# A third buffer for the gathered rows of y, R shared out anew over the periods, and x1's zero padding on VectorE

## The chip, the cores and the metric

The kernel runs on one core of a Trainium2 chip. A core has five engines with a queue of instructions each: TensorE (PE in the profile; its weight loads, PEld, overlap the products), VectorE (DVE), ScalarE (ACT), GpSimd (POOL) and SyncE (SP, which here only issues transfers). They meet through semaphores. Transfers run on 16 DMA engines. The metric is the time of one execution in microseconds; the time before is the median of three runs, 1281.5 (1278.85 to 1284.95).

## The reference, cut to what matters

```python
# x: 2708 x 256, adj: 2708 x 2708, some 0.3% of it nonzero, float32
x  = layernorm(x + relu(concat([x, adj @ x]) @ weight + bias))        # layer 0
R  = adj + eye(2708);  R = R / R.sum(-1, keepdims=True)               # layer 1
Z, Xf, Xa = 0, x, x
for n in range(2):
    A  = top_p_attention(Xa, W1, W2, W3)   # softmax of (Xa W1' W2') (Xa W3')'; of each row
                                           # the largest 0.9 of the mass, scaled to sum 1
    Xf = R @ Xf
    Xa = A @ Xa
    Z  = Z + Xf @ U1[n].T + Xa @ U2[n].T
x  = layernorm(x + layernorm(x + Z))
```

So there are two dense attention steps, A of 2708 x 2708 each time, and a chain of two products with the sparse R. Since R(R x) U1[1]' + (R x) U1[0]' = R (R (x U1[1]') + x U1[0]'), the kernel first forms yf = x U1[1]' and v0 = x U1[0]', then v = R yf + v0, then R v, which goes into the sum.

## The kernel before, in words

**Blocks.** The 2708 rows are 22 blocks (NB) of 128; the last one (EDGE) has 20 rows. The 2708 columns of A or adj are turned and multiplied in chunks of 128.

**Layer 0** (to about 265 us) multiplies adj by x on TensorE, block by block (L266), and leaves x1, the layer's result, in SBUF. Meanwhile DVE and POOL make for each block a list of the columns of adj that hold a nonzero: at most 896, seven chunks of 128. `Lists.end` closes such a round: DVE orders the marks (up to L350), POOL writes them to memory, scatters them by seven indirect transfers (L354) and reads the list `ix` back (L357). There are two rounds, one before step 1 and one within it; for each block only the listed rows of adj' are then kept (adjc in memory, 7 chunks of 128 columns, and the block's own 128 x 128 piece).

**Just after the first round** stand two instructions for the last block of x1: POOL zeroes a 128 x 256 tile, `x1_edge` (L508), and DVE copies the 20 rows of x1 into it (L509). The products of step 1 read it as the 22nd chunk (`part_y`, L583), the first time at the last slot of turn 0. Then follow POOL's memset of `sums` (L603), read by `finish1`.

**Step 1** is a software pipeline over blocks t. Logits of a block (PE L527) go through one PSUM buffer and are copied to one of four row buffers `e` by ACT (L534). DVE takes each segment's largest 8 (`extract1`, L589) and sorts them; ACT takes exponentials (`exps1`: first of the sorted values, L630, then of the row); DVE finds the threshold and zeroes what lies below (`finish1`, L654). `begin1` starts three blocks, with `u1_project` between, which makes yf and v0 with TensorE and U1, copies them out on ACT (L673) and stores them; it is the last reader of U1. Then the loop over t runs: in six slots each four transposes of `e` (PE L554, copied by ACT L556) and four products with x1 (PE L583), with exps1(t+2), finish1(t+1), logits and extract1 of t+3 beside them. The step's result goes on to q, k and za in memory; `ya_pair` (PE L691) makes ya = Xa U2[1]' at the end, and the first three blocks' logits of step 2 stand there too.

**Step 2** is a loop over periods `per` from 0 to 23 of six slots. In a period PE turns and multiplies block per-2 (again L554 and L583, now with ya), DVE searches the top-p threshold of blocks per and per-1 (L1045 is the one pass that ends the search's first part, L1110 the mask that releases the block to PE), ACT makes passes for block per+1 and exponentials of block per+2 (logits again L527). Everything is issued in the order of the code; each engine runs its own part in that order.

**R** is done within step 2, in units. One unit is one product of a chunk (PE L769), eight to a block: seven chunks of gathered rows and the block's own 128 rows. There are 176 units for yf (s = 0) and 176 for v (s = 1). `units` says how many go into each period: 16 first, 8 each in periods 0 and 1, 18 in each of 2 to 9, none in 10, 16 in each of 11 to 21. With a block's first unit `r_load` asks for the next block: adj's chunks by two SP transfers into one of three `adj` tiles (`a_load`), seven indirect gathers on POOL (`y_load`, L739), one chunk of 128 rows of 256 floats each, into the one of two buffers `yg` that the block before used, and the own rows by an SP transfer into the eighth place of the same buffer. The first two blocks' gathers are issued earlier, in the last-but-one turn of step 1 (`y_at`). With s = 0 the result is scaled and added by DVE (L797) and stored to v; after the last block v is complete and the gathers of s = 1 can start. With s = 1 the result is added to za (`arrive`).

**The finals.** A block whose three parts have arrived goes through two layernorms, `Final`, two blocks at a time (`final_slot`): statistics on DVE (L1204), roots on ACT (L1241), the first norm on ACT (L1214) into one of four spare tiles, then gain and x1 added on POOL (L1229, L1230), and a slot later statistics again. The last blocks, in `tail`, use DVE in POOL's place.

**Room.** One SBUF tile of 128 x 5416 floats, `y_room`, holds the two buffers of y (8 chunks each), the four spare tiles, and `x1_edge`.

Of the kernel before, what the change touches and what calls it, by code (L numbers as in the profile page):

```python
# [20 lines left out]
P = 128  # L21
# [18 lines left out]
ML = 16  # L40
CW, CC = 128, 7
AT = 96
# [19 lines left out]
def gnn_two_layer_kernel(ctx: ExitStack, tc: tile.TileContext, N, xT_d, x_d, adj_d, w0_d, b0_d,  # L62
# [45 lines left out]
    c.adj_d, c.out_d = adj_d, out_d  # L108
# [50 lines left out]
def fast_path(ctx, tc, c, flags, fint, xT_d, x_d, w0_d, b0_d, w1_d, w2_d, w3_d, u1_d, u2_d, g_d, b_d):  # L159
# [344 lines left out]
    YW = 2 * (CC + 1) * D  # L504
    yg = y_room[:, :YW].rearrange("p (s c d) -> p s c d", s=2, d=D)
    spares = [y_room[:, YW + D * i:YW + D * (i + 1)] for i in range(4)]
    x1_edge = y_room[:, YW + 4 * D:YW + 5 * D]
    nc.gpsimd.memset(x1_edge, 0.0)  # L508
    nc.vector.tensor_copy(x1_edge[AT:AT + rows(EDGE)], x1[:rows(EDGE), EDGE, :])  # L509
    lists = Lists(ML, NB, flags[:, NF - 2:], yg[:, 1].rearrange("p c d -> p (c d)"))  # L510
# [224 lines left out]
    def y_load(s, m):  # L735
        y = yg[:, m % 2]
        rows_d = (c.yf_d, c.v_d)[s].rearrange("p k d -> (p k) d")
        for i in range(CC):
            nc.gpsimd.indirect_dma_start(out=y[:CW, i, :], out_offset=None, in_=rows_d,  # L739
                                         in_offset=bass.IndirectOffsetOnAxis(ap=ix[:CW, m, i:i + 1], axis=0))  # L740
        y_in[s, m] = y
# [7 lines left out]
    def r_load(s, m):  # L749
        if m not in a_in:  # L750
            a_load(m)
        if (s, m) not in y_in:
            y_load(s, m)
        y = y_in.pop((s, m))
        nc.sync.dma_start(out=y[:rows(m), CC, :], in_=(c.yf_d, c.v_d)[s][:rows(m), m, :])
        r_in[s, m] = a_in.pop(m), y

    def r_units(n):
        for _ in range(n):
            s, m = r_queue[0]  # L760
            p = rows(m)
            if not r_now:
                r_now[:] = [ps_misc(), 0]
                if m + 1 < NB:
                    r_load(s, m + 1)
            acc, k = r_now
            a, y = r_in[s, m]
            kw = CW if k < CC else p
            nc.tensor.matmul(acc[:p, :D], lhsT=a[:kw, k, :p], rhs=y[:kw, k, :], start=k == 0, stop=k == CC)  # L769
# [24 lines left out]
    def r_out(s, m, acc, base):  # L794
        p = rows(m)
        if s == 0:
# [3 lines left out]
            if m == NB - 1:  # L800
                r_load(1, 0)
        else:
# [111 lines left out]
    y_at = {(NB - 2, 2): 0, (NB - 2, 5): 1}  # L914
    stores = []
    blocks = {}
    for t in range(NB):
# [5 lines left out]
        ra_next = finish1(t + 1) if t + 1 < NB else None  # L923
        for g in range(NG):
# [31 lines left out]
            if (t, g) == (NB - 1, 2):  # L956
                a_load(0)
# [6 lines left out]
    r_load(0, 0)  # L964
    for f in ends:
# [313 lines left out]
    first = 2 * (CC + 1)  # L1279
    units = {0: CC + 1, 1: CC + 1}  # L1280
# [117 lines left out]
def general_path(ctx, tc, c):  # L1398
# [15 lines left out]
    ps = ctx.enter_context(tc.tile_pool(name="gps", bufs=2, space=PSUM))  # L1414

# [341 lines left out]
```

## Time and profile before

| | |
|---|---|
| median of 3 runs | 1281.5 us (1278.85 to 1284.95) |
| the profiled execution: its time, its span | 1286.8, 1284.9 us |
| TensorE clock granted, mean | 0.975 |
| busy: PE, PEld | 1202.1 (94%), 904.3 us (70%) |
| busy: DVE, ACT, POOL | 973.9 (76%), 735.1 (57%), 634.9 us (49%) |
| gathers L739, yf and v | 154 each: 190.7 and 193.5 us busy, 48.3 and 59.3 idle before them |
| products of R, L769 | 704 records: 187.9 us busy, 18.1 idle before them |
| DMA | 165.99 MB, mean 129 GB/s |
| first transpose of step 1; R's first gather from step 2; end | 347.6; 744.4; 1284.9 us |

Times are microseconds from the start of the span. In a timeline a row is one instruction, or a run of like ones (x16): its start, its length, engine, line, operation, what it writes and reads, and in brackets the idle time of its engine before it with the instruction or transfer that ended it. A row of busy times by stretch gives the stretch, its length, the busy time and number of instructions of PE, PEld, DVE, ACT and POOL, then the granted clock, the DMA engines' share and GB/s. "issue" is idle time that no wait in the records explains.

### The profile page before, as it was taken

What the parts mean: (1) busy time and instruction counts of PE and PEld (TensorE: products, weight loads), DVE (VectorE), ACT (ScalarE), POOL (GpSimd) and SP (SyncE); (2) the same over time, 40 slices, a digit from 0 to 9 for tenths busy, and PEclk for the clock granted to TensorE, in tenths of its full rate; (3) what the DMA queues carried; (4) which work ended last, traced back from release to release, by engine and by line L of the source; (5) the groups of instructions that cost most, each with busy time, mean ns of one, the idle gap of its engine ahead of it and who ended that gap; (6) DMA issues with size and microseconds to landing.
All of it is one profiled execution on the core that took longest, in us unless ns stands there. A gap on an engine that the chain in (4) does not pass through costs nothing.

```text
span 1284.9 us, 18709 instructions
## 1 busy us (share of the span) xinstructions
PE 1202.1 (94%) x5772; PEld 904.3 (70%) x5772; DVE 973.9 (76%) x3253; ACT 735.1 (57%) x1299; POOL 634.9 (49%) x597
## 2 busy tenths in 40 slices
PE   8999999987799999999999978999998999999885
PEld 6888888842377777777777646777766777776664
DVE  2455554973999998988871278979878999999886
ACT  2000111032566666666665498887888999989821
POOL 1000000004076552577766068878774878888860
PEclk9999999989899999999999888999999999999997
DMA  7455544523322220133334154665664555555451
GB/s 197 149 197 172 160 151 153 172 82 98 100 80 92 61 68 32 41 94 94 91 89 107 50 152 152 181 187 178 183 150 122 173 160 163 169 185 160 144 135 39
DMA packets 101703, 165.99 MB, mean 129 GB/s; under 512 B 17362, under 2 KB 74070, under 8 KB 101594
## 3 DMA queue, kind: packets, MB, share of 16 engines
q1 hardware_dynamic: 75308, 108.65, 26.1%
q0 software_dynamic: 20544, 51.17, 14.8%
q10 hardware_dynamic: 5742, 4.89, 1.3%
q8 instruction: 48, 0.79, 0.3%
q14 instruction: 61, 0.50, 0.1%
HBM read 130.74 MB, written 33.90 MB: 128 GB/s over the span
## 4 chain that ended last, share of the span: by engine, by line
PE 71%; DVE 10%; ACT 7%; DMA 6%; issue 3%; POOL 2%; SPq 0%; POOLq 0%; ACTq 0%; DVEq 0%
PE acc L583 23%; PE acc L266 16%; PE lg L527 8%; PE misc L769 6%; PE tr L554 6%; DMA yg<-yf_d,ix 3%; PE acc L670 2%; DMA yg<-v_d,ix 2%; DVE e L1110 2%; PE misc L402 2%; ACT e L988 2%; PE acc L691 2%; PE misc L441 2%; PE misc L719 2%; PE acc L477 1%
## 5 line engine op out<-in xcount | busy, mean ns | idle before, releaser
L556 ACT COPY wT<-tr 128x512 f32<-128x512 f32 (+2 forms) x258 | 136.6, 537 | 205.8 <-PE tr L554 205.8
L583 PE MATMUL acc<-ya,wT 128*128 128x256 f32 x924 | 223.1, 383 | 0.0
L739 POOL DMA_INDIRECT yg<-v_d,ix x154 | 193.5, 1256 | 59.3 <-issue 25.3
L583 PE MATMUL acc<-x,wT 128*128 128x256 f32 x882 | 217.4, 386 | 0.0
L739 POOL DMA_INDIRECT yg<-yf_d,ix x154 | 190.7, 1239 | 48.3 <-issue 26.2
L266 PE MATMUL acc<-y,adj_t 128*128 128x257 f32 x924 | 206.1, 382 | 0.0
L769 PE MATMUL misc<-yg,adj_t 128*128 128x256 f32 (+1 forms) x704 | 187.9, 398 | 18.1 <-DMA yg<-yf_d,ix 7.2
L583 PEld LDWEIGHTS acc<-x,wT 128*128 128x128 f32 x882 | 159.0, 190 | 58.1 <-issue 24.7
L583 PEld LDWEIGHTS acc<-ya,wT 128*128 128x128 f32 x924 | 172.1, 191 | 38.2 <-issue 16.7
L266 PEld LDWEIGHTS acc<-y,adj_t 128*128 128x128 f32 x924 | 174.9, 191 | 27.3 <-issue 1.9
L376 POOL DMA_INDIRECT adj_t<-in_adj,ix x154 | 168.4, 1094 | 50.9 <-issue 39.5
L769 PEld LDWEIGHTS misc<-yg,adj_t 128*128 128x128 f32 (+1 forms) x704 | 123.6, 191 | 69.6 <-issue 23.2
L527 PE MATMUL lg<-k,q 64*128 64x512 f32 (+3 forms) x528 | 138.0, 600 | 27.4 <-ACT e L534 13.5
L554 PE MATMUL tr<-ident,e 128*128 128x128 f32 (+1 forms) x946 | 145.2, 272 | 6.9 <-ACT wT L556 4.6
L554 PEld LDWEIGHTS tr<-ident,e 128*128 128x128 f32 (+1 forms) x946 | 117.7, 141 | 40.5 <-ACT wT L556 8.8
L343 POOL DMA_DIRECT2D part_d<-e x1 | 0.6, 573 | 278.6 <-DVE e L342 278.6
L988 ACT ACTIVATE e<-e,st 128x2708 f32<-128x2708 f32 (+1 forms) x43 | 113.5, 2640 | 0.1
L991 ACT ACTIVATE e<-e,st 128x2708 f32<-128x2708 f32 (+1 forms) x42 | 111.0, 2642 | 0.1
L454 ACT COPY x1T<-tr 128x256 f32<-128x256 f32 (+1 forms) x22 | 8.0, 365 | 179.8 <-PE tr L453 179.8
L589 DVE MAX8 cand<-e 128x8 f32<-128x170 f32 (+1 forms) x352 | 86.9, 318 | 15.9 <-ACT e L534 15.7
L1052 DVE MAX8 cand<-w 128x8 f32<-128x170 f32 (+1 forms) x352 | 94.1, 321 | 0.0
L527 PEld LDWEIGHTS lg<-k,q 64*128 64x128 f32 (+1 forms) x528 | 39.3, 183 | 59.1 <-issue 20.7
(246 smaller groups left out, 1749.6 us busy)
## 6 DMA issues: line engine op xcount, KB each, us to landing
adj_t<-in_adj SPq DMA_DIRECT2D x44, 704.0 KB
adj_t<-adjc_d SPq DMA_DIRECT2D x44, 448.0 KB
adjc_d<-adj_t SPq DMA_DIRECT2D x22, 256.0 KB
base<-za_d SPq DMA_DIRECT2D x40, 128.0 KB
adjc_d<-adj_t SPq DMA_DIRECT2D x22, 192.0 KB
xt<-in_x ACTq DMA_DIRECT2D x21, 128.0 KB
x_d<-x SPq DMA_DIRECT2D x21, 128.0 KB
x1b_d<-xb SPq DMA_DIRECT2D x21, 128.0 KB
```

The costliest lines, as they stand in the source:

```text
L266: nc.tensor.matmul(acc[:p, :n], lhsT=halves[k // KH][:, k % KH, :p], rhs=y[:, k, :n], start=k == 0, stop=stop and k == NB - 1)
L376: nc.gpsimd.indirect_dma_start(out=a[:CW, i, :], out_offset=None, in_=adj_rows, in_offset=bass.IndirectOffsetOnAxis(ap=ix[:CW, m, i:i + 1] ...
L527: nc.tensor.matmul(lg[:p, h, at:at + b - a], lhsT=q[o, t * P:t * P + p], rhs=keys[s][o, i, :b - a], start=True, stop=True)
L554: nc.tensor.transpose(tr[:, k % 4, :p], columns(e[:p], k), ident[:p, :p])
L556: nc.scalar.copy(wT[:, :len(ks), :p], tr[:, :len(ks), :p])
L583: nc.tensor.matmul(acc[:p, :D], lhsT=wT[:, k % 4, :p], rhs=part_y(y, k), start=k == 0, stop=k == NB - 1)
L589: nc.vector.max(dst[:p, i * 8:(i + 1) * 8], src[:p, i * step:i * step + w])
L739: nc.gpsimd.indirect_dma_start(out=y[:CW, i, :], out_offset=None, in_=rows_d, in_offset=bass.IndirectOffsetOnAxis(ap=ix[:CW, m, i:i + 1], ...
L769: nc.tensor.matmul(acc[:p, :D], lhsT=a[:kw, k, :p], rhs=y[:kw, k, :], start=k == 0, stop=k == CC)
L988: nc.scalar.activation(scr[:b.p, :N], e, AF.Relu, bias=b.nz, scale=b.l[k], accum_out=b.relu)
L991: nc.scalar.activation(scr[:b.p, :N], e, AF.Sign, bias=b.nz, scale=b.l[k], accum_out=b.sign)
L1052: nc.vector.max(b.cand[:p, 8 * i:8 * i + 8], low[:p, SEG2 * i:SEG2 * (i + 1)])
```

## The change

- `yg` has three buffers of seven chunks instead of two of eight. With a block's first unit `r_load` asks for the block after the next. The own rows go to free chunks of the block's adj tile (chunks 8 and 9 of its 11), so `r_in` holds three things.
- The four spare tiles of the finals and `x1_edge` lie in U1's place, which step 1 leaves after `u1_project`. The kernel's other path (`general_path`, which is taken only when a list or a search overflows) loads U1 again.
- x1_edge's zeros are a DVE memset and stand, with the copy, in turn 0 of step 1 behind finish1(1).
- The gathers of the first three blocks of yf are issued in step 1, at other slots, and the first two adj loads there too; at the hand-over from s = 0 to s = 1 two blocks are asked for instead of one.
- Units: 24 first, 8 in period 0, 16 in period 1, 16 in each of periods 2 to 9, none in 10, 16 in each of 11 to 21.

```diff
--- before.py
+++ after.py
@@ -105,7 +105,7 @@
 
     c = Common()
     c.N, c.D, c.DA, c.NB, c.DC, c.KH, c.CHS, c.rows = N, D, DA, NB, DC, KH, CHS, rows
-    c.adj_d, c.out_d = adj_d, out_d
+    c.adj_d, c.out_d, c.u1_d = adj_d, out_d, u1_d
     c.x1_d = dram.tile([N, D], FP, name="x1_d")
     c.x1b_d = dram.tile([N, D], FP, name="x1b_d")
     c.za_d = dram.tile([N, D], FP, name="za_d")
@@ -501,13 +501,12 @@
     assert not weights
     lists.end()
     y_room = big.tile([P, DC * N], FP, tag="Y", name="yg")
-    YW = 2 * (CC + 1) * D
-    yg = y_room[:, :YW].rearrange("p (s c d) -> p s c d", s=2, d=D)
-    spares = [y_room[:, YW + D * i:YW + D * (i + 1)] for i in range(4)]
-    x1_edge = y_room[:, YW + 4 * D:YW + 5 * D]
-    nc.gpsimd.memset(x1_edge, 0.0)
-    nc.vector.tensor_copy(x1_edge[AT:AT + rows(EDGE)], x1[:rows(EDGE), EDGE, :])
-    lists = Lists(ML, NB, flags[:, NF - 2:], yg[:, 1].rearrange("p c d -> p (c d)"))
+    YW = CC * D
+    yg = y_room[:, :3 * YW].rearrange("p (s c d) -> p s c d", s=3, d=D)
+    idle = [c.u1[:, j, i, :] for j in range(DC) for i in range(2)]
+    spares = list(idle)
+    x1_edge = idle[0]
+    lists = Lists(ML, NB, flags[:, NF - 2:], y_room[:, YW:])
     lists.turn()
     x1_transpose(NB - 1)
     x1_qk(len(CHS) - 1)
@@ -733,7 +732,7 @@
     ready = []
 
     def y_load(s, m):
-        y = yg[:, m % 2]
+        y = yg[:, m % 3]
         rows_d = (c.yf_d, c.v_d)[s].rearrange("p k d -> (p k) d")
         for i in range(CC):
             nc.gpsimd.indirect_dma_start(out=y[:CW, i, :], out_offset=None, in_=rows_d,
@@ -751,9 +750,10 @@
             a_load(m)
         if (s, m) not in y_in:
             y_load(s, m)
-        y = y_in.pop((s, m))
-        nc.sync.dma_start(out=y[:rows(m), CC, :], in_=(c.yf_d, c.v_d)[s][:rows(m), m, :])
-        r_in[s, m] = a_in.pop(m), y
+        a, y = a_in.pop(m), y_in.pop((s, m))
+        own = a[:, CC + 1:CC + 1 + D // P, :].rearrange("p c i -> p (c i)")
+        nc.sync.dma_start(out=own[:rows(m)], in_=(c.yf_d, c.v_d)[s][:rows(m), m, :])
+        r_in[s, m] = a, y, own
 
     def r_units(n):
         for _ in range(n):
@@ -761,12 +761,13 @@
             p = rows(m)
             if not r_now:
                 r_now[:] = [ps_misc(), 0]
-                if m + 1 < NB:
-                    r_load(s, m + 1)
+                if m + 2 < NB:
+                    r_load(s, m + 2)
             acc, k = r_now
-            a, y = r_in[s, m]
+            a, y, own = r_in[s, m]
             kw = CW if k < CC else p
-            nc.tensor.matmul(acc[:p, :D], lhsT=a[:kw, k, :p], rhs=y[:kw, k, :], start=k == 0, stop=k == CC)
+            nc.tensor.matmul(acc[:p, :D], lhsT=a[:kw, k, :p], rhs=y[:kw, k, :] if k < CC else own[:p],
+                             start=k == 0, stop=k == CC)
             r_now[1] += 1
             if k == CC:
                 r_now.clear()
@@ -799,6 +800,7 @@
             nc.sync.dma_start(out=c.v_d[:p, m, :], in_=base[:p])
             if m == NB - 1:
                 r_load(1, 0)
+                r_load(1, 1)
         else:
             arrive(m, base, acc, rinv[:p, m:m + 1])
 
@@ -911,7 +913,7 @@
 
     at = {(m // 2, 3 * (m % 2) + 1): m for m in range(4)}
     at.update({(m - 2, 3): m for m in range(4, NB)})
-    y_at = {(NB - 2, 2): 0, (NB - 2, 5): 1}
+    y_at = {(NB - 3, 5): 0, (NB - 2, 3): 1, (NB - 1, 1): 2}
     stores = []
     blocks = {}
     for t in range(NB):
@@ -921,6 +923,9 @@
         if t >= NB - 3:
             b = blocks[t - (NB - 3)] = Block(t - (NB - 3))
         ra_next = finish1(t + 1) if t + 1 < NB else None
+        if t == 0:
+            nc.vector.memset(x1_edge, 0.0)
+            nc.vector.tensor_copy(x1_edge[AT:AT + rows(EDGE)], x1[:rows(EDGE), EDGE, :])
         for g in range(NG):
             turn(t, g, x1, acc, es[t % 4])
             if ends and 1 <= g <= 3:
@@ -953,8 +958,8 @@
             if (t, g) in y_at:
                 name_y()
                 y_load(0, y_at[t, g])
-            if (t, g) == (NB - 1, 2):
-                a_load(0)
+            if t == NB - 1 and 1 < g < 4:
+                a_load(g - 2)
         if t == EDGE:
             products(0)
             acc = edge_sum(acc, D, meanwhile=ya_pair)
@@ -962,6 +967,7 @@
         ra = ra_next
     assert not stores and not staged and not to_turn
     r_load(0, 0)
+    r_load(0, 1)
     for f in ends:
         ya_pair()
         f()
@@ -1276,8 +1282,8 @@
 
 
     each = NB * (CC + 1)
-    first = 2 * (CC + 1)
-    units = {0: CC + 1, 1: CC + 1}
+    first = 3 * (CC + 1)
+    units = {0: CC + 1, 1: 2 * (CC + 1)}
     rest = each - first - sum(units.values())
     units.update({p: rest * (p - 1) // 8 - rest * (p - 2) // 8 for p in range(2, 10)})
     units.update({p: each * (p - 10) // 11 - each * (p - 11) // 11 for p in range(11, 22)})
@@ -1413,6 +1419,9 @@
     small = ctx.enter_context(tc.tile_pool(name="gsmall", bufs=4))
     ps = ctx.enter_context(tc.tile_pool(name="gps", bufs=2, space=PSUM))
 
+    for s in range(2):
+        nc.sync.dma_start(out=u1[:, :, s, :], in_=c.u1_d[s].rearrange("(c p) e -> p c e", p=P))
+
     def ps_lg():
         return ps.tile([P, CH], FP, tag="lg", name="lg")
```

## Prediction

> **What bounds the kernel now.** I read, in this order: the busy slices and the chain of the page, the list of waits, the timelines of DVE, ACT, PE and POOL at 262–366 us and from 680 us on, and the busy time of the engines by period of step 2. TensorE is busy 94% of the span and holds 71% of the chain, so what counts is where it waits, and where it has more to do than the stage's other limit. Two places stand out.
>
> The first is the start of step 1, here in the timelines of POOL, DVE, ACT and PE (start, length, work, idle time before it and what ended that):
>
> ```profile
> 309.63 1.24 POOL L357 DMA_DIRECT2D ix<-list_d  x1 [1.41 <-DMA list_d<-e,to]
> 310.86 0.32 POOL L508 MEMSET yg<- 128x256 f32 x1
> ...
> 311.22 0.56 DVE L509 COPY yg<-x 20x256 f32<-20x256 f32 x1 [19.58 <-POOL xs L603]
> 311.79 3.88 DVE L589 MAX8 cand<-e 128x8 f32<-128x170 f32 x16
> ...
> 321.22 0.35 ACT L630 ACTIVATE srt<-srt,nmax 128x65 f32<-128x65 f32 x1 [12.88 <-DVE srt L596]
> ...
> 325.33 2.08 PE L527 MATMUL lg<-k,q 64*128 64x512 f32 x4 [12.96 <-ACT e L534]
> ```
>
> The zeroing L508 stands on POOL behind the first list's seven scatters (L354) and the read L357, which go one by one and end at 310.87. DVE has nothing else before its copy L509 and waits 19.6 us; its sort for block 0 (L589) comes after; ACT waits 12.9 us for the sort; PE waits 13.0 us for ACT to empty the one logits buffer.
>
> The second place is R in step 2. In POOL's timeline every gather L739 takes 0.95 and has 0.30 us before it, from 744 to 1245 us:
>
> ```profile
> 744.44 0.95 POOL L739 DMA_INDIRECT yg<-yf_d,ix  x1 [1.68 <-PE misc L769]
> 745.70 0.94 POOL L739 DMA_INDIRECT yg<-yf_d,ix  x1 [0.30 <-PE misc L769]
> ...
> 797.91 3.22 POOL L739 DMA_INDIRECT yg<-yf_d,ix  x1 [0.30 <-DMA yg<-yf_d,ix]
> ...
> 960.59 0.95 POOL L739 DMA_INDIRECT yg<-yf_d,ix  x1 [0.30 <-issue]
> 975.50 0.94 POOL L739 DMA_INDIRECT yg<-v_d,ix  x1 [13.97 <-DMA v_d<-base]
> ...
> 1042.82 0.73 POOL L1229 TENSOR_TENSOR yg<-yg,gb 128x256 f32<-128x256 f32 x1 [2.15 <-ACT yg L1214]
> ...
> 1241.07 0.73 POOL L1229 TENSOR_TENSOR yg<-yg,gb 128x256 f32<-128x256 f32 x1
> ```
>
> POOL stands still only at the hand-over from yf to v (14.0 us) and once before L1229 (2.15). It never waits for a free buffer. A gather costs 1.25 us, and two in each period (like that at 797.91) meet DVE's passes L1110 and L1045 and cost some 2.35 more. The stretches, by first transpose of a period (length, then busy PE, PE loads, DVE, ACT, POOL):
>
> ```profile
> 801.90:825.00 23.10, 23.10 (x115) 18.16 (x114) 20.95 (x77) 19.89 (x32) 18.53 (x16) 1.00 0.56 170
> 825.00:970.60 145.60, 141.55 (x679) 105.02 (x678) 121.94 (x418) 119.48 (x192) 109.72 (x89) 1.00 0.59 170
> 970.60:991.30 20.70, 17.02 (x84) 11.99 (x82) 16.57 (x52) 19.82 (x32) 12.44 (x12) 1.00 0.51 153
> 1013.60:1035.90 22.30, 22.30 (x112) 17.46 (x111) 20.91 (x75) 20.29 (x34) 18.04 (x15) 1.00 0.56 173
> ```
>
> Row 1 is a period with 18 units of R and nothing missing: PE needs 23.1. Row 2 is six more such periods of 24.3 each: POOL's 15.75 gathers x 1.25 + 2 x 2.35 = 24.4. Row 4 has 16 units: PE needs 22.3. From about 1130 us on POOL sets the pace again, through L1229/L1230 for which DVE waits:
>
> ```profile
> 1217.71 0.43 DVE L1204 BATCH_NORM_STATS2 bst<-yg 128x6 f32<-128x256 f32 x1 [2.15 <-POOL yg L1230]
> 1242.63 0.43 DVE L1204 BATCH_NORM_STATS2 bst<-yg 128x6 f32<-128x256 f32 x1 [2.77 <-POOL yg L1230]
> ```
>
> **Part 1, x1's zeros.** POOL loses one memset (0.32). DVE's sort can start when L350 is done and block 0's logits are copied, at 291.7 instead of 311.8, and ends at 301.1. ACT reaches L630 after its own copies, whose last one (L673) ends at 308.34: it starts there and not at 321.22, 12.8 us sooner. From there the order is a chain (ACT's exponentials, DVE's finish1 and second sort, ACT, the last projections, the first transpose at 347.57), each link as long as before, and step 1 is PE without a gap (34.0 busy of 34.0 in five stretches). So **-12.8** reaches step 2. PE's own wait shrinks to some 0.2 us. The `sums` memset L603, behind the same scatters, is done at 311.2 against a need at 311.6, so it doesn't bite; if it did, fractions of a us.
>
> The zeroing and copy come back in turn 0: a DVE memset of that size takes 0.27 (L182), the copy 0.56. They stand behind finish1(1), which ends near 352.4, after PE's last read of U1 (347.6), so their new wait is empty; if it weren't, block 3's sort and, through it, turn 3 would be late. Need for x1_edge: 364.7. Cover: finish1(1) is ready 10 us ahead of its turn. Without it, +0.8. Taken: 0. Spares in U1's place, own rows in adj's tile and the reload in the general path (not entered) change no instruction's size or number here. The waits for a free buffer on SP (own rows, 101 us in all, its longest 16.4) pass to adj's loads: behind them stand za's and v's stores and x1b's loads, but each load is now asked for two blocks (some 20 us) ahead, and PE waited only once for adj (0.97). Taken: 0; from 0 to +2.
>
> **Part 2, R anew.** *Before R.* Seven more gathers go out at 703.7 in POOL's 39 us of idle time: 7 x 1.25 = 8.8, hidden. Units move from periods 2–9 (18 to 16) into the opening burst (16 to 24) and period 1 (8 to 16), where ACT's passes set the pace. DVE's products of the burst now number three and wait for PE until 754, about 3.6 us later than now; ACT doesn't need them.
>
> *Where it pinches.* POOL's stream from 744.4 is saturated either way, so gather j now stands where gather j-7 stood. The end of period 1 takes 48 units, gather 42: the present 35th, issued at 776.6, landing near 780 (landings: median 3.6 after issue). Period 2's first five chunks are the present 36th to 40th, the last issued at 785.4, landing near 788.6; PE wanted them at about 783. So the logits behind them come at 789 instead of 783.6, +5.5. Two units fewer by then bring period 3 to 806.5 against 801.9: **+4.6** (from 0, if landings are quick, to +7).
>
> *Periods 3–9.* POOL could do 14 x 1.25 + 2 x 2.35 = 22.2, PE needs 22.3: seven periods at 22.3 = 156.1 against 168.7: **-12.6**. Two limits so close together cost something; I add +1 (0 to 4). Period 10 starts **7.0** sooner. Its 20.7 and the 14-us hand-over stay, since the last product, DVE's L797 and the store of v follow as now.
>
> *The way back.* In the second product POOL's order becomes 49 gathers, then the first L1229, where it was 42: +7 x 1.25 = 8.75, less the 2.15 of idle time that goes, = **+6.6**. So the first L1229 pair stands at 1042.8 - 7.0 + 6.6 = 1042.4, as now, though DVE arrives sooner: it waits about 2 us for the pair in period 13 and is bound to POOL from there. The pairs keep their 24.8 us (14 gathers, 4 x 0.75, two slow ones). Up to 1219 us nearly all of the 7 is gone: **-0.4**.
>
> *Tail.* After the eighth pair only 7 gathers remain instead of 14; PE's waits for chunks at 1224–1234 and DVE's 2.77 + 0.84 at 1242 go. Period 21 takes about 21.5 (DVE busy 21.0) instead of 24.9: **-3.4**.
>
> **Two rules weighed.** Row: gathers of 3.2 where others take 0.95. The Trainium skill, "SBUF — State Buffer", section "Who interferes with whom": DVE with two SBUF inputs and a GpSimd instruction that reads SBUF share a port, and the second blocks until the first is done. L1110 and L1045 have two such inputs, a gather reads its list. Counted as full passes of 3.05, POOL would need 14 x 1.25 + 2 x 3.05 = 23.6 in periods 3–9, and those would yield -3.5 rather than -12.6; period 10 would even start late and the sum be -6. The six periods of row 2 bear out 2.35, which I take. The skill's first page ("Trainium Kernel Development and Optimization", "Best Practices") has buffering hide transfers behind compute; by it PE's 14.4 us of waits for gathers would all go on top of -12.8, a sum of -27. The rows speak against it: a producer that never waits for a buffer gains only a head start.
>
> **Sum:** -12.8 - 0.4 - 3.4 = -16.6. Profiled: span 1284.9, execution 1286.8, so 1.9 lie around it. 1286.8 - 16.6 = 1270.2; the execution shown is 5.3 above the median of 1281.5, so against that **1265**. No change and change are told apart here from about 0.5%, 6.4 us.
>
> **Rivals.**
> - *Gathers land early enough* (0.22): no stall in period 2. For it: POOL's lead of six gathers today at 780; against: that lead is what the move spends. Period 10 11.6 sooner instead of 7.0: -21, about 1260; with a lighter coupling of POOL and DVE 1256.
> - *Step 2 gives nothing* (0.25): landings of up to 6.3 us and POOL's 22.2 against PE's 22.3 make PE stall; period 10 only 2 sooner, so +4.6 at the eighth pair and -3.4 after it. -12.8 + 1.2: about 1270; 1274 with period 10 unmoved and a smaller tail.
> - *The zeros were not the cause* (0.06): DVE still waits near 291, for a list transfer that the view names badly. Against: L350 ends at 291.6. Only -3.8: 1278.
> - *Slower* (0.04): a ring in periods 13–20. L1230 late, so DVE's mask late, PE late, the buffer of three blocks ago late, POOL idle, the next L1230 later still. It decides once POOL stands still over 2.9 us in each of eight periods, 23 us in all: from there the time passes 1288, say 1290. Against: that buffer is released about a period before its gather.
>
> **Numbers.** 0.43 for 1265 and the rest as given. The middle case alone spans 1261 to 1269. Range 1255 to 1276: the two neighbours with their bounds, leaving out the last two cases and the far edges. Faster 0.89, same 0.07, slower 0.04.
>
> **What would show it.** Part 1: no DVE wait before the first sort, the first transpose near 334.8, step 2's R near 730.7. Part 2: in period 2 a PE wait for gathers of some 5 us; periods 3–9 at 22.3 to 22.6; the hand-over's POOL gap still near 14; L1204 waiting for L1230 from the first pair on, pairs 24.8 apart; no PE wait for gathers after 1150. I'd be wrong if periods 3–9 stay near 24, if pairs come closer than 24.8, or if the first transpose moves by less than 12.

## The result, and the profile after

| | before | after |
|---|---|---|
| median, us | 1282.3 (1278.9 to 1285.0) | 1268.4 (1264.8 to 1270.3) |
| ratio after / before | | 0.9891, 95% interval 0.9863 to 0.9920 |
| profiled execution: its time, its span | 1286.8, 1284.9 | 1264.8, 1263.0 |
| granted TensorE clock, mean | 0.975 | 0.987 |

The kernel became 13.9 us faster; 1265 was forecast. The two profiled executions differ by 21.9 us, more than the medians, because that of before lay 5 us above its median and that of after 4 us below its own; a second trace of the changed kernel, taken beside the experiments, has a span of 1265.7. Two of the four sets of experiments ran where the kernel before itself takes 1326 us and ACT, in the traces, stands still for up to 28.6 us with no wait in the records that explains it; kernels from there are compared only with each other.

The start of step 1, in the timelines of POOL, DVE, ACT and PE of the changed kernel (start, length, work, idle time before it and what ended that), and the same two rows of PE in the kernel before:

```profile
306.63 1.24 POOL L357 DMA_DIRECT2D ix<-list_d  x1 [1.40 <-DMA list_d<-e,to]
307.87 0.11 POOL L602 MEMSET xs<- 128x1 f32 x1
...
288.73 0.21 DVE L350 SCALAR_TENSOR_TENSOR to<-run,before_m,e 16x7 int32<-16x7 f32 x1
288.87 3.86 DVE L588 MAX8 cand<-e 128x8 f32<-128x170 f32 x16
...
307.60 0.35 ACT L629 ACTIVATE srt<-srt,nmax 128x65 f32<-128x65 f32 x1
...
328.49 5.46 PE L669 MATMUL acc<-u,x1T 128*128 128x512 f32 x8 [4.20 <-ACT v_out L672]
333.87 0.66 PE L553 MATMUL tr<-ident,e 128*128 128x128 f32 x4
```

```profile
342.11 5.46 PE L670 MATMUL acc<-u,x1T 128*128 128x512 f32 x8 [2.40 <-ACT v_out L673]
347.50 0.66 PE L554 MATMUL tr<-ident,e 128*128 128x128 f32 x4
```

DVE goes from the list (L350) straight into the sort; its 19.6 us of waiting there are gone (it waits 10.2 for ACT's exponentials later), and so are ACT's 12.9 ahead of the exponential (L629 now) and PE's 13.0. The list itself is nearly as late as it was (L357 ends at 307.87 instead of 310.87): DVE, ACT and PE no longer stand behind it. The first transpose stands at 333.9 instead of 347.5.

Step 2 by stretches (length, busy PE, PE loads, DVE, ACT, POOL, granted clock, DMA share, GB/s): period 3, periods 4 to 9, period 10, period 12, period 14 of the changed kernel:

```profile
790.85:813.24 22.39, 22.39 (x112) 17.35 (x111) 18.19 (x64) 19.88 (x32) 18.12 (x15) 1.00 0.60 182
813.24:946.68 133.44, 133.44 (x657) 102.13 (x656) 119.63 (x413) 119.33 (x192) 98.63 (x79) 1.00 0.56 160
946.68:967.33 20.65, 16.98 (x84) 11.96 (x82) 18.27 (x60) 19.78 (x32) 11.25 (x10) 1.00 0.54 173
989.64:1011.92 22.28, 22.28 (x112) 17.45 (x111) 20.89 (x75) 20.28 (x34) 18.02 (x15) 1.00 0.57 174
1036.92:1061.08 24.16, 22.77 (x111) 17.29 (x111) 22.08 (x80) 22.27 (x38) 19.87 (x19) 1.00 0.55 170
```

Periods 4 to 9 take 133.44 / 6 = 22.24 us and PE is busy for all of it; before they took 24.3. From period 14 on a period is 24.2 us with PE busy 22.8. POOL's timeline around the hand-over from yf to v, at the finals' first pair and at their eighth, and two of DVE's waits, show what paces that part:

```profile
934.69 0.95 POOL L738 DMA_INDIRECT yg<-yf_d,ix  x1 [0.30 <-issue]
953.34 0.94 POOL L738 DMA_INDIRECT yg<-v_d,ix  x1 [17.70 <-PE tr L553]
...
1027.99 0.75 POOL L1235 TENSOR_TENSOR u<-u,gb 128x256 f32<-128x256 f32 x1
...
1197.96 0.73 POOL L1235 TENSOR_TENSOR u<-u,gb 128x256 f32<-128x256 f32 x1
...
1029.57 0.43 DVE L1210 BATCH_NORM_STATS2 bst<-u 128x6 f32<-128x256 f32 x1 [3.40 <-POOL u L1236]
1031.07 0.43 DVE L1210 BATCH_NORM_STATS2 bst<-u 128x6 f32<-128x256 f32 x1 [0.86 <-POOL u L1236]
```

POOL stands still for 17.7 us at the hand-over (14.0 before), then for no more than 0.43 us at a time until its last gather at 1213.1, and DVE waits for the finals' additions (L1236) from the first pair on.

### The profile page after: what moved, and what is told of

It reads as the page before. It is cut to its first block, busy times and chain, and to the rows that moved or that the text cites. A ratio compares the mean times of both kernels' runs of the same rounds, so it can differ in the third digit from the quotient of the medians.

```text
span 1263.0 us, 18675 instructions
## 1 busy us (share of the span) xinstructions
PE 1191.0 (94%) x5772; PEld 901.6 (71%) x5772; DVE 969.5 (77%) x3254; ACT 734.8 (58%) x1299; POOL 631.5 (50%) x596
## 4 chain that ended last, share of the span: by engine, by line
PE 79%; DVE 9%; POOL 4%; ACT 3%; issue 2%; DMA 2%; ACTq 0%; POOLq 0%; DVEq 0%
PE acc L582 27%; PE acc L266 16%; PE lg L526 9%; PE misc L769 8%; PE tr L553 7%; DVE e L1116 3%; POOL yg L738 3%; PE acc L669 2%; PE misc L402 2%; DVE w L1111 2%; PE acc L690 2%; PE misc L441 2%; PE misc L718 2%; DMA yg<-yf_d,ix 1%; PE acc L477 1%
## 5 line engine op out<-in xcount | busy, mean ns | idle before, releaser
L738 POOL DMA_INDIRECT yg<-v_d,ix x154 | 190.8, 1239 | 63.2 <-issue 27.7
L582 PEld LDWEIGHTS acc<-ya,wT 128*128 128x128 f32 x924 | 173.3, 192 | 38.6 <-issue 16.7
L769 PE MATMUL misc<-yg,adj_t 128*128 128x256 f32 (+1 forms) x616 | 162.0, 392 | 12.1 <-DMA yg<-yf_d,ix 11.5
L769 PEld LDWEIGHTS misc<-yg,adj_t 128*128 128x128 f32 (+1 forms) x616 | 106.5, 188 | 54.2 <-DMA yg<-yf_d,ix 17.5
L588 DVE MAX8 cand<-e 128x8 f32<-128x170 f32 (+1 forms) x352 | 86.6, 317 | 15.2 <-ACT e L533 15.1
L1111 DVE MATCH_REPLACE8 w<-part,e 128x680 f32<-128x680 f32 (+1 forms) x88 | 74.4, 851 | 0.0
```

The costliest lines, as they stand in the source:

```text
L582: nc.tensor.matmul(acc[:p, :D], lhsT=wT[:, k % 4, :p], rhs=part_y(y, k), start=k == 0, stop=k == NB - 1)
L1111: nc.vector.match_replace(w[:b.p, W * i:W * (i + 1)], b.part[:b.p, i, :], e2(b.t)[:b.p, W * i:W * (i + 1)], 3.0e38)
```

## The experiments

### The zeros alone

The kernel before, with only this:

```diff
-    nc.gpsimd.memset(x1_edge, 0.0)
-    nc.vector.tensor_copy(x1_edge[AT:AT + rows(EDGE)], x1[:rows(EDGE), EDGE, :])
...
         ra_next = finish1(t + 1) if t + 1 < NB else None
+        if t == 0:
+            nc.vector.memset(x1_edge, 0.0)
+            nc.vector.tensor_copy(x1_edge[AT:AT + rows(EDGE)], x1[:rows(EDGE), EDGE, :])
```

> Only x1's zeros and copy are moved to DVE in turn 0; the rest is the kernel before. Theory: the first transpose of step 1 comes 12.8 to 13.6 us sooner (334 instead of 347.5) and, with step 2 as before, the whole of it reaches the end: 1282.3 - 13 = 1269. That is also where the changed kernel stands (1268.4), so if this holds by the medians, R's new sharing adds little; if step 2 adds what the two profiles show (8 us), this one stands 5 to 8 us above the changed kernel. Rival (zeros not the cause): 1278 or more, DVE still waits near 291 us.

Measured: 1271.2 against 1281.7, a ratio of 0.9919 (0.9895 to 0.9943), or -10.5 us. In the trace the first transpose stands at 336.1 instead of 347.5, R's first product at 730.5 instead of 743.5, and the end at 1271.5 instead of 1284.9: 11.4 us of gain at the first transpose, 13.0 at R's start, 13.5 at the end. So the wait was the zeros', and what they gave stayed to the end. Against the 13.9 of the whole change this leaves some 3 us for everything else.

### Buffers and units, each without the other

Two kernels stand with the zeros alone and the changed kernel in a square. The first is the changed kernel with two buffers and a lead of one block:

```diff
-        y = yg[:, m % 3]
+        y = yg[:, m % 2]
...
-                if m + 2 < NB:
-                    r_load(s, m + 2)
+                if m + 1 < NB:
+                    r_load(s, m + 1)
...
-                r_load(1, 1)
...
-    y_at = {(NB - 3, 5): 0, (NB - 2, 3): 1, (NB - 1, 1): 2}
+    y_at = {(NB - 2, 2): 0, (NB - 2, 5): 1}
...
-            if t == NB - 1 and 1 < g < 4:
-                a_load(g - 2)
+            if (t, g) == (NB - 1, 2):
+                a_load(0)
...
-    r_load(0, 1)
```

> The changed kernel with two buffers in turn and a lead of one block, the new units and all else kept. Theory (the new units gain, not the buffer): periods 3 to 9 at 22.3 to 23 us each, period 10 at most 5 us later than in the changed kernel, 1268 to 1273. Rival (the lead is what matters): PE waits for gathers in every period, periods near 24, POOL idle at each block's start, 1276 or more.

The second keeps the third buffer and takes the units of before:

```diff
-    first = 3 * (CC + 1)
-    units = {0: CC + 1, 1: 2 * (CC + 1)}
+    first = 2 * (CC + 1)
+    units = {0: CC + 1, 1: CC + 1}
```

> The changed kernel with the units of before (16 first; 8, 8, then 18 in periods 2 to 9) and the third buffer kept. Theory: periods 3 to 9 go back to 24.3 each since POOL needs 15.75 x 1.25 + 4.7, the wait in period 2 goes, so period 10 starts some 10 us later than in the changed kernel, and POOL, which never rests from the hand-over to the last block, hands that on to the end: about 1278. Rival (the buffer's lead is the gain): within 3 us of the changed kernel, 1268 to 1271.

The changed kernel itself ran beside them:

> The changed kernel again, for a second trace beside the experiments on the same chip: 1265 to 1271; period 10 at 946 to 950, POOL's gap at the hand-over 17 to 18, no idle time on POOL from there to 1213.

Measured, all on one chip, with the stretches of the traces from R's first product to period 3 and on to period 10:

| kernel | buffers, units | ratio to before | R to period 3 | periods 3 to 9 | sum |
|---|---|---|---|---|---|
| before | two, old | 1 | 58.4 | 168.8 | 227.2 |
| zeros alone | two, old | 0.9919 (0.9895 to 0.9943) | 57.5 | 169.4 | 226.9 |
| two buffers | two, new | 0.9933 (0.9912 to 0.9955) | 73.5 | 155.7 | 229.2 |
| units of before | three, old | 0.9895 (0.9863 to 0.9928) | 58.3 | 161.5 | 219.9 |
| changed kernel | three, new | 0.9900 (0.9867 to 0.9933) | 63.8 | 156.8 | 220.6 |

The first trace of the changed kernel has 63.9, 155.8 and 219.8. The intervals of the ratios of the last four kernels overlap, so by the medians nothing in R is told apart from the zeros alone; the traces tell two buffers from three, by far more than the 0.8 us between the two traces of the changed kernel. The new units do what they say, shorter periods 3 to 9, and pay for it ahead of them: with two buffers 16 us more before period 3 for 13.7 less after it. The third buffer is worth 7 to 9 us by period 10 with either set of units. The expectation for two buffers came true in its periods (22.2 each), not in period 10, which stands 8.6 us later after R's first product than in the changed kernel, where at most 5 was expected. That for the units of before was wrong: periods of 24.3 and about 1278 were expected, 23.1 and 1268.0 were measured. The two stretches of that kernel, then of the zeros alone (columns as above):

```profile
731.47:789.80 58.33, 44.19 (x187) 32.18 (x186) 50.51 (x171) 53.21 (x80) 44.55 (x37) 0.88 0.56 170
789.80:951.33 161.53, 161.53 (x793) 124.42 (x792) 141.31 (x487) 139.26 (x224) 120.16 (x97) 1.00 0.57 169
```

```profile
730.49:788.02 57.53, 45.53 (x187) 32.27 (x186) 50.52 (x171) 53.18 (x80) 45.59 (x37) 0.88 0.56 168
788.02:957.38 169.36, 164.88 (x793) 123.15 (x792) 143.06 (x494) 139.31 (x224) 128.30 (x104) 1.00 0.59 170
```

With the third buffer PE is busy for all of 161.53 us, 23.1 a period, the 18 units' own need; with two it stands still for 4.5 and is slower in what it does. Yet POOL, at 18 units a period, needs 24.3. It is behind PE's pace there and doesn't show it, since it started seven gathers ahead.

### The third buffer without its head start

If that is so, the gain is not in the lead of two blocks but in when the first gathers go out:

```diff
-    y_at = {(NB - 3, 5): 0, (NB - 2, 3): 1, (NB - 1, 1): 2}
+    y_at = {(NB - 3, 5): 0, (NB - 2, 3): 1}
```

The third block's seven gathers then stand behind step 1, with R's first unit. All else is the changed kernel.

> The changed kernel with three buffers, the lead of two blocks and the new units; only the third block's seven gathers are not issued within step 1 but with R's first unit. POOL then has 140 gathers from there to the hand-over instead of 133. Theory (POOL never rests from R's start to the last gather of yf, so what the third buffer gives is the seven gathers that it lets go out in POOL's idle time before): the last gather of yf stands about 216 us after R's first unit instead of 208, period 10 some 7 to 9 us later than in the changed kernel, and the time at 1271 to 1275, like two buffers. Rival (the lead itself keeps PE from waiting): as the changed kernel, 1266 to 1269.

Measured: 1275.8 against 1280.6, a ratio of 0.9966 (0.9952 to 0.9981), outside the changed kernel's intervals and a little more than the 1271 to 1275 expected. It is also above the zeros alone (0.9919): without those seven gathers in POOL's idle time the rest of R's change loses by the end. From R's first product to period 10 it takes 226.0 us, against 219.8 and 220.6; the last gather of yf stands 212.8 after R's first product, against 207.8 and 208.6, not quite the 216 expected. POOL's timeline where step 1 ends, of the changed kernel and then of this one:

```profile
697.81 0.95 POOL L738 DMA_INDIRECT yg<-yf_d,ix  x1 [0.30 <-issue]
726.05 0.11 POOL L985 MEMSET e<- 128x12 f32 x1 [27.29 <-PE acc L690]
...
727.89 0.95 POOL L738 DMA_INDIRECT yg<-yf_d,ix  x1 [1.68 <-PE misc L769]
730.98 0.94 POOL L738 DMA_INDIRECT yg<-yf_d,ix  x1 [2.14 <-PE misc L769]
```

```profile
691.17 0.94 POOL L738 DMA_INDIRECT yg<-yf_d,ix  x1 [0.30 <-issue]
729.59 0.11 POOL L985 MEMSET e<- 128x12 f32 x1 [37.48 <-PE acc L690]
...
730.28 0.95 POOL L738 DMA_INDIRECT yg<-yf_d,ix  x1 [0.53 <-issue]
```

The changed kernel uses 10 us of POOL's idle time, 37.5 down to 27.3, for gathers that otherwise join a queue that doesn't rest until the hand-over. It gives some of that back at once: it waits 1.68 and 2.14 us for PE in R's first 4 us, where the other issues without a pause from 730.28 on. That is most of why seven gathers of 1.25 us move the last one by 4.2 to 5.0 and not by 8.75. Same buffers, same lead, same units: up to period 10 the head start is worth 5.4 to 6.2 us. The lead is worth less, and not nothing: two buffers with the same units take 229.2, this kernel 226.0. The last gather of yf comes 3.2 us sooner as well: 1.2 because POOL starts sooner, 2.0 because the slow gathers cost less.

### The hand-over

POOL's gap at the hand-over had been forecast to stay at 14 us and grew. The last block of the first product was finished sooner, first so:

```diff
-                later[1].append(lambda s=s, m=m, acc=acc, base=base: r_out(s, m, acc, base))
+                later[0 if (s, m) == (0, NB - 1) else 1].append(lambda s=s, m=m, acc=acc, base=base: r_out(s, m, acc, base))
...
             n = n_r * (g + 1) // NG - n_r * g // NG
+            if per == 9:
+                n = (2, 3, 3, 3, 5, 0)[g]
```

> The changed kernel, with the last block of the first product finished sooner: in period 9 the units are shared 2, 3, 3, 3, 5, 0 over the slots instead of 2, 3, 3, 2, 3, 3, and that block's scaling and store stand one slot after its last product instead of two. Theory (POOL's stream after the hand-over sets the end): the first gather of v comes 4 to 8 us sooner, POOL's gap shrinks from 17.7 to 10 to 13, and the end by as much: 1260 to 1264. Rival (PE or DVE set the end, POOL's stream only keeps up): the gather comes sooner, the end within 2 us: 1266 to 1270.

That kernel ran where the kernel before takes 1326.0: 1334.4, a ratio of 1.0050 (1.0030 to 1.0071), with no run of the changed kernel beside it, so it says nothing of the hand-over. The second form, with the scaling also ahead of DVE's mask pass, ran where before stands at 1280.6:

```diff
+            if (per, g) == (9, NG - 1):
+                while now:
+                    now.pop(0)()
             next(vector)
```

> The changed kernel, with the last block of the first product finished sooner: period 9 shares its units 2, 3, 3, 3, 5, 0 over the slots, and that block's scaling and store stand one slot after its last product, ahead of DVE's mask pass. Theory (POOL's stream after the hand-over sets the end): the first gather of v stands 7 to 9 us sooner after the last one of yf (10 instead of 18.6), and the end comes 6 to 8 us sooner than in the changed kernel: 1260 to 1262, a ratio of 0.983 to 0.985. Rival (PE and DVE set the end): the gather comes sooner, the end within 2 us of the changed kernel, 1266 to 1270.

Measured: 1265.5, a ratio of 0.9889 (0.9865 to 0.9912): not told apart from the changed kernel, and less than the 0.983 to 0.985 expected. The traces say why. DVE's scaling of the last block (L798) in the changed kernel, behind a pass of 3 us that stands between it and its product:

```profile
947.80 3.03 DVE L1051 SCALAR_TENSOR_TENSOR w<-e,st 128x2720 f32<-128x2720 f32 x1
950.76 0.08 DVE L1051 DVE_READ_ACCUMULATOR w<-e,st 128x1 f32 x1
950.76 0.47 DVE L798 SCALAR_TENSOR_TENSOR base<-misc,rinv,base 20x256 f32<-20x256 f32 x1
```

and DVE's and POOL's timelines with the sooner hand-over:

```profile
944.31 0.47 DVE L798 SCALAR_TENSOR_TENSOR base<-misc,rinv,base 20x256 f32<-20x256 f32 x1 [3.75 <-PE misc L769]
...
936.09 0.95 POOL L738 DMA_INDIRECT yg<-yf_d,ix  x1 [0.30 <-issue]
946.99 3.69 POOL L738 DMA_INDIRECT yg<-v_d,ix  x1 [9.95 <-PE tr L553]
...
953.48 2.90 POOL L738 DMA_INDIRECT yg<-v_d,ix  x1 [0.30 <-issue]
```

The gap shrinks from 17.7 to 9.95. But from the first gather of v to the finals' first pair POOL now takes 79.4 us instead of 74.65: two more gathers, those at 946.99 and 953.48, meet DVE's passes and take 3.69 and 2.90, 4.7 us that the old gap had covered. Measured from R's first product the first pair stands 4.7 to 5.6 us sooner, the end 2.4 to 5.2. So the end follows POOL's stream in these traces, by 2.4 to 5.2 of the 6 to 8 us expected; but the changed kernel's own two traces differ by 2.8 there, and the medians don't show it.

### The order of the second product, and the finals' additions

With a lead of one block in the second product only:

```diff
-                if m + 2 < NB:
-                    r_load(s, m + 2)
+                if m + 2 - s < NB:
+                    r_load(s, m + 2 - s)
...
-                r_load(1, 1)
```

> The changed kernel, with the lead of two blocks kept in the first product only; in the second product gathers are asked for one block ahead as before. Theory of the prediction (the finals' first pair pays 7 x 1.25 - 2.15 = 6.6 us for standing behind seven more gathers, and the tail gives 3.4 back): the first pair stands some 7 us sooner after the hand-over (67 us instead of 74.7), periods 13 and 14 return to 22.3 and 23.2, the tail gets longer, the end 3 us sooner: 1265. Rival (POOL never rests from the hand-over to its last gather, so the order of its work moves nothing): 67 us for the pair too, but the end within 2 us of the changed kernel, 1266 to 1270.

> The changed kernel, with a lead of one block in the second product only, once more on a chip where the kernel before stands near 1281. Theory of the prediction (standing behind seven more gathers costs the finals' first pair 6.6 us and the tail gives 3.4 back): the first pair 66 to 67 us after the first gather of v instead of 74.7, from the first gather to the end 307 us instead of 310 to 312 (as in the kernel with two buffers), the time 3 us below the changed kernel, 1264 to 1266, a ratio of 0.987. Rival (POOL never rests, so the order of its work moves nothing): the pair sooner too, but the end within 1.5 us of the changed kernel, 0.9885 to 0.9905.

With the finals' addition on DVE:

```diff
         def stats(self, i):
             p, self.i = self.p, i
+            if self.add:
+                self.add = False
+                nc.vector.tensor_tensor(self.h[:p], self.h[:p], self.x1[:p], op=ALU.add)
...
-            nc.gpsimd.tensor_tensor(h[:p], h[:p], self.x1[:p], op=ALU.add)
+            self.add = True
```

> The changed kernel, with the finals' addition of x1 taken from POOL (two of 0.73 us in each period from 13 on) to DVE, just ahead of the statistics. Theory (POOL paces periods 14 to 20 at 24.1 us): they shorten to about 23.0, DVE's 22.1 + 0.9, and the end comes 6 to 9 us sooner: 1259 to 1262. Rival (DVE paces them, its waits for POOL only fill its slack): periods 24.5 to 25, 1271 to 1275.

Two kernels combine: the additions with the hand-over's first form, and the lead of one block with its second form.

> The additions on DVE and the sooner hand-over together. If POOL paces everything after the hand-over, the two gains add up until PE's 22.8 us a period binds: 1253 to 1258. If only one of them pays, it stands where that one stands; if DVE paces, at 1266 or more.

> The lead of one block in the second product and the sooner hand-over together. If the order of POOL's work costs 3 us and the sooner hand-over is worth the 2 to 5 us that it showed from R's first unit to the end: 1259 to 1263, a ratio of 0.983 to 0.986, ahead of both kernels. If only the hand-over pays: as it stood, 0.988 to 0.989.

All of these ran where the kernel before takes 1326 us:

| kernel | median of all runs, us | ratio to before there, fast runs | first gather of v | first pair | end, in the trace |
|---|---|---|---|---|---|
| lead of one block, first run | 1339.9 | 1.0109 (1.0079 to 1.0138) | 1017.4 | 1097.8 | 1339.4 |
| the same, second run | 1342.4 | 1.0110 (1.0049 to 1.0170) | 1016.8 | 1096.6 | 1338.6 |
| hand-over, first form | 1334.4 | 1.0050 (1.0030 to 1.0071) | 1011.2 | 1091.9 | 1332.0 |
| additions on DVE | 1347.8 | 1.0112 (1.0051 to 1.0174) | 1015.2 | 1094.5 | 1348.9 |
| additions and hand-over | 1341.6 | 1.0109 (1.0077 to 1.0141) | 1010.4 | 1090.8 | 1337.6 |
| lead and hand-over, second form | 1334.2 | 1.0061 (1.0034 to 1.0088) | 1007.4 | 1091.0 | 1334.2 |

*The lead.* It can't be read here: between the first gather and the first pair falls a period of 29 to 36 us (period 12, or period 11 with the hand-over's first form), stretched by idle time that none of the kernel's waits explains. What hint there is comes from the kernels measured elsewhere. From the first gather of v to the first pair, those with the old order in the second product take 65.9 to 67.3 us, those with the new one 74.6 to 74.9. To the end the old order takes 307.2 (two buffers), 309.2 (zeros alone) and 309.4 (before); the new one 309.7 and 311.7 (the changed kernel's two traces), 309.9 (no head start) and 310.5 (units of before). So the pair comes some 8 us sooner with the old order and the end, on the mean, 1.8. The prediction works out 3.2 (6.6 - 3.4). With a spread of 2 us among traces of the same order, it stays open.

*The hand-over here.* Lead and hand-over against the lead alone, second run: first gather of v 9.5 us sooner, end 4.4 sooner in the traces, 0.5% by the medians' ratios. But its stretched period 12 is also 5.8 us shorter (28.8 against 34.6), so this shows no more of the hand-over's worth.

*The additions.* Against the hand-over's first form alone, which differs in nothing else, they cost 7.2 us by the medians and 5.7 in the traces. POOL has less to do and is not the faster for it. Of the lists of waits, the rows for POOL, first without and then with the additions on DVE (engine, what is late and for whom, us in total, times, longest):

```profile
POOL u L1235 <- ACT u L1220: 15.1, 1, 15.1
```

```profile
POOL u L1239 <- ACT u L1224: 40.2, 6, 19.4
```

POOL's multiplication (L1235, L1239 with the edit) now waits for ACT's norm six times instead of once. The one of 15.1, and two of the six (19.4 and 9.5), lie behind POOL's last gather; of the others the longest are 6.5 and 4.2 us. And by the busy times of periods 16 to 19 DVE works 92.4 of 96.7 us against 89.5 of 94.9. In the kernel with the additions alone, periods 16 to 19 take 27.1 us, more than the 24.5 to 25 of the rival. So work taken from POOL went to an engine with 5.4 us to spare in four periods, and POOL, which had not waited for ACT there, then did. That these waits form a ring over DVE, ACT and POOL, as in the prediction's last rival, is likely and not shown.

No kernel was clearly faster than the changed one. Whether the change itself gains where before takes 1326 was not measured; the kernels nearest to it, with another order in the second product or another hand-over, were 0.5 to 1.1% slower than before there.

## Why the prediction was right, and where it wasn't

**Part 1, forecast -12.8 (rival: not the cause).** Right, in its mechanism too. The zeros alone gave 10.5 us by the medians (7.3 to 13.5 by the interval) and 13.0 at R's start in the trace. The chain's links are "each as long as before": from ACT's first exponential to the first transpose it is 26.28 us before (321.22 to 347.50), 26.27 now (307.60 to 333.87) and 26.31 with the zeros alone. In that last trace the first transpose moved by 11.4 and not by 12, which the prediction had named as a sign of being wrong; the difference lies ahead of the chain, whose start at 309.74 differs by 2.1 between that execution and the changed kernel's. What the prediction left out is off that chain. PE had been slow as well as idle: four logits products take 2.08 us before where the usual is 1.13, and a run of eight projections 4.56 where it is 3.70, 1.8 us more. Two stretches of the kernel before, ahead of PE's 13.0 us of idle time and just after it (columns as above, the granted clock third from the end):

```profile
308.66:312.30 3.64, 3.64 (x10) 1.44 (x8) 1.07 (x4) 0.00 (x0) 2.00 (x8) 1.00 0.37 88
325.33:327.40 2.07, 2.07 (x5) 0.57 (x5) 1.97 (x5) 0.91 (x2) 0.00 (x0) 0.50 0.33 111
```

The Trainium skill, "TensorE: Matmul & The Clock Gate", Part 1, says the clock is halved after an idle window and restored by sustained work; the records agree with that: 1.00, then 13.0 us of idle time, then 0.50. The 1.8 us of slow products are gone now, and PE's next wait, before the last projections, grew by as much, from 2.4 to 4.2: PE didn't set the pace there, ACT and DVE did, so the faster clock gave nothing more.

**Part 2 up to period 10, forecast -7.0.** The sum holds, measured from R's first product: 219.8 and 220.6 against 227.2, -7.4 and -6.6. So do its terms: +4.6 at period 3 was +5.5 (63.9 against 58.4), -12.6 for periods 3 to 9 was -12.9 (155.8 against 168.8), and the +1 between two close limits did not come (0.7 in the second trace). What was wrong is whose gain it is. "Seven more gathers go out at 703.7 in POOL's 39 us of idle time: 7 x 1.25 = 8.8, hidden" was entered at nothing, and the gain put down to the units, by PE's 22.3 against POOL's 22.2. Without those seven gathers the same units gain 1.2 (226.0), and with two buffers they lose 2.0 (229.2); with the gathers and the old units 7.3 come (219.9). The prediction used the head start one paragraph on ("gather j now stands where gather j-7 stood"), but only to find where it pinches; it didn't ask what the old units would gain from it, and that was as much. Work moved from a queue that never rests into its idle time shortens the queue: here 7 x 1.25 = 8.75 at most, of which 5.4 to 7.3 reach period 10. The remark that "a producer that never waits for a buffer gains only a head start" was right, and the head start was most of the gain. So the sum for this part came right in part by luck, with its gain under the wrong name; that the new units and the old ones come out within 1 us of each other was not foreseen.

**The hand-over, forecast to stay at 14.0.** It took 17.7. Both kernels wait there for PE's last units, and for DVE, which has a pass of 3 us between the product and the scaling; POOL, seven gathers ahead, arrives earlier and waits longer. By the distance from period 10 to the first gather of v, 6.7 us against 4.9, this costs 1.8.

**The way back, forecast +6.6 at the first pair, then pairs 24.8 us apart.** From the first gather of v to the first pair 74.65 us against 67.3: +7.3. Right. But the seven intervals to the eighth pair take 170.0 us, 24.3 each, against 173.3. The reason is in the slow gathers: the first of the two in a period takes about 2.6 us in six of seven now and 2.6 to 3.8, mostly over 2.9, before, so it meets DVE's pass in another phase. The seven sum to 19.3 us against 22.7, which is the whole difference. By the sum the eighth pair was to stand 13.2 us sooner, and it stands 18.2 sooner. That is the largest miss of a size, 5 us, in the profiled execution. Of it 3.7 are there already at R's start: it was to come 12.8 sooner and came 16.5 sooner, at 727 in both traces of the changed kernel, where those of the other kernels in these two sets, whose code is the same or nearly so up to there, have 730 to 731.5. Why step 1, from its first transpose to R's first product, is 1.4 to 2.8 us shorter in those two than in the others stays open.

**The tail, forecast -3.4.** From the eighth pair to the end 68.8 us before, 65.1 and 67.1 in the two traces after: -3.7 and -1.8. PE's waits for v's gathers are gone from the list of waits, as forecast. Period 21 takes the 21.5 forecast; its length before, by first transposes, is 23.1 (1226.5 to 1249.7), not 24.9, so less of the tail's gain lies in that period than was put there.

**The total.** -12.8 - 0.4 - 3.4 = -16.6 was forecast, 13.9 came, with an interval of 10.3 to 17.6. By one chip's medians the zeros gave 10.5 of it (forecast 12.8) and the rest 3.4 (forecast 3.8), though medians with intervals of 3 us on each side don't carry that to a tenth. The rival "step 2 gives nothing" (1270, period 10 only 2 us sooner) came close in time (1268.4) and not in its mechanism: measured from R's start, period 10 is 7 sooner, and part is given back after it. "Gathers land early enough" falls: period 2 waited, 3.9 us of PE's time in the first trace.

**The rule weighed.** Full passes of 3.05 for each collision would make periods of 23.6 at 14 gathers. Two gathers that meet the same DVE pass one period apart stand at 859.63 and 881.92, 22.3 apart with 14 gathers between, so the two collisions cost (22.3 - 17.5) / 2 = 2.4 each. The row was right, and a full pass too dear by 0.65 each. Yet what the prediction quotes, that the second waits until the first is done, agrees with the traces. One gather of each kind with the DVE pass that it met:

```profile
858.67 3.03 DVE L1051 SCALAR_TENSOR_TENSOR w<-e,st 128x2720 f32<-128x2720 f32 x1
859.63 2.90 POOL L738 DMA_INDIRECT yg<-yf_d,ix  x1 [0.30 <-issue]
...
875.25 3.04 DVE L1116 SCALAR_TENSOR_TENSOR e<-w,st,e 128x2720 f32<-128x2720 f32 x1
875.33 3.79 POOL L738 DMA_INDIRECT yg<-yf_d,ix  x1 [0.30 <-PE tr L553]
```

The passes end at 861.70 and 878.29, the gathers 0.83 later in both cases. In the traces of before and after, each of the 41 slow gathers ends 0.81 to 0.83 us after the pass. So a gather loses what is left of the pass when it starts, 0.1 us less: 1.95 us for the first of these, 2.84 for the second. Counting whole passes was the error in applying the rule. (The prediction's -6 for this case is too small: its own terms, -12.8 + 4.6 - 3.5 + 6.6 - 3.4, make -8.5, or -7.5 with its 1 for two close limits.)

## What to carry to other kernels

Where one engine's queue never rests for a long stage, look at what that engine does before the stage: each instruction moved into idle time there can shorten the stage by up to its own length (here 5.4 to 6.2 us came of 8.75), and a buffer more was worth having for that more than for the lead (3.2). A line of a prediction that says "hidden, costs nothing" should be read once more as a gain: what queue would it otherwise stand in? Taking load off a saturated engine pays only as long as the engine that takes it has room for it and if the first doesn't then wait for it.

## What the runs showed of the hardware

- In two of the four sets this program stands still where no record explains it, at the same places or a period apart. ACT before the exponentials of a block in period 1, in one kernel of each of these sets:

```profile
813.99 1.11 ACT L865 ACTIVATE e<-lg,nmax 128x1024 f32<-128x1024 f32 x1 [28.64 <-remote]
```

```profile
813.57 1.11 ACT L866 ACTIVATE e<-lg,nmax 128x1024 f32<-128x1024 f32 x1 [27.69 <-remote]
```

"remote" means that the records name nothing that released it. From R's first product to period 2 these kernels take 63 to 64 us, the changed kernel 39 to 41 elsewhere. The chip on record is number 7 for one of these sets and number 3 for the other, but number 3 also for the set in which before takes 1280.6, so it isn't shown that the chip makes the difference. The cause stays open. A gain of 1% found in one set is not safe in another.

- A gather on POOL that starts within a DVE pass of 3.04 us with two inputs in SBUF ends 0.81 to 0.83 us after the pass, in all 41 cases of each of the two profiles, and takes 2.5 to 3.8 us instead of 0.95. One that started before the pass, or with it to 0.01 us, is not slowed: 33 such in the changed kernel took 0.94 to 0.95. A stream of gathers that starts earlier may meet more passes: the sooner hand-over lost 4.7 of its 9.4 to 10.3 us to two of them.
